# Three staggered streams, per-batch norms and early-divided attention in a four-layer graph network

## The chip, the cores and the metric

The kernel runs on one core of a Trainium2 chip. The metric is device time in microseconds (us) of one execution. Five engines matter below: TensorE (PE; its weight loads are listed apart as PEld), VectorE (DVE), ScalarE (ACT), GpSimd (POOL), and SyncE (SP), which issues the transfers of x and of the result. Each has its own queue of instructions. TensorE has a granted clock, shown as a share of full speed. All timed runs quoted here are in the fast state.

## The reference, cut to what matters

128 batches of 128 nodes with 512 features go through four layers. Each is `x = layernorm(x + layer(x))`, with a shared 128 x 128 matrix `adj`:

```python
# layer 0
y = einsum('nm,bmd->bnd', adj, x);  out = y @ weight + bias
# layer 1: graph attention, one head
h = x @ W
e = leaky_relu((h @ a1)[:, :, None] + (h @ a2)[:, None, :]) * adj
out = elu(softmax(e) @ h + beta * h)
# layer 2: with adj for both weights this reduces to one maximum per row
out = max over m of relu((adj @ x)[o, m] + b[o])
# layer 3: attention with 8 heads of 64, masked where adj == 0
q, k, v = x @ w_qkv
o = softmax(q k^T / 8 + mask) v @ w_proj + b_proj
out = o + (layernorm(o) * gamma + beta3)
```

Everything is fp32. The layer norm is a mean, a variance, and a power of -0.5.

## The kernel before

A group is four batches. `front` takes a group through layers 0 to 2, `back` through layer 3, and the two are stepped in turn, so that two neighbouring groups are in flight. The parts that the argument touches (cuts marked `# ...`):

```python
def interleave(*runs):
    runs = [r for r in runs if r is not None]
    while runs:
        runs = [r for r in runs if next(r, StopIteration) is not StopIteration]

def mean_rstd(st):                      # all four batches of a group at once
    mv = small.tile([P, G, 2], F32, name="mv")
    for b in range(G):
        nc.vector.bn_aggr(mv[:, b, :], st[:, b, :])
    ve = small.tile([P, G], F32, name="ve")
    nc.vector.tensor_scalar(ve, mv[:, :, 1], EPS, None, op0=ALU.add)
    rstd = small.tile([P, G], F32, name="rstd")
    nc.gpsimd.tensor_tensor(rstd, ve, neghalf, op=ALU.pow)
    return mv, rstd

# front, layer 1: scores as 32 products with two columns, mixing after the product
ps = ps_mm.tile([P, G, 2], F32, name="mm")
for b in range(G):
    for k in range(K):
        nc.tensor.matmul(ps[:, b, :], xT[:, k, b * P : (b + 1) * P], wa[:, k, :], ...)
# ... softmax of the four batches' weights e; h = x @ w1; eT = e transposed
for b in range(G):
    p = ps_mm.tile([P, D], F32, name="mm")
    nc.tensor.matmul(p, eT[:, b, :], h[:, b, :], start=True, stop=True)
    # ... elu, residual, stats
mv, rstd = mean_rstd(st)
for b in range(G):
    normalised(xs[:, b, :], xs[:, b, :], mv, rstd, b)

# back, layer 3: one exponential for all heads; the division comes after the values
nc.vector.tensor_tensor(pr, pr, nmx[:, :, None].to_broadcast([P, H, P]), op=ALU.add)
nc.scalar.activation(pr, pr, AF.Exp)
# ... pr transposed to prT
for j in range(2):
    for c in range(K):
        nc.tensor.matmul(pov[:, j, c, :], prT[:, j * K + c, :], ve[:, 2 * c + j, :], ...)
nc.vector.reciprocal(rs, pov[:, :, :, HD : HD + 1])   # sums from a column of ones
nc.vector.tensor_tensor(oa..., pov[:, :, :, :HD], rs..., op=ALU.mult)
transposed(oT, oa, 0)

last = None
for g in range(NG):
    interleave(last, front(xs))
    last = back(g, xs)
```

## Time and profile before

| Before | value |
|---|---|
| time, median of 3 runs | 5197.13 us (5194.22 to 5197.48) |
| span of the profiled run | 5207.6 us |
| TensorE busy / idle | 4181.9 / 1025.7 us |
| TensorE waits that the trace names | 1001 us |
| TensorE time at half clock | 1113 us |
| period of one group | about 161 us |

How to read it: TensorE leads, but it is idle for a fifth of the span, and a fifth of its span runs at half clock. The two go together: after a wait of several microseconds its next products are slow. Time at half clock counts all time at that clock, idle included. The page's lines, the two stretches and the chain are shown in the prediction below. One more place of the timeline matters for later (columns: start, length, engine, line, operation, tile out<-in, shapes, count):

```profile
2727.08 3.63 PE L209 MATMUL mm<-wa,xT 128*128 128x2 f32 x32
...
2731.27 2.08 PE L168 MATMUL mm<-xT,wqkv_sb 128*128 128x512 f32 x2
```

The 32 two-column products follow one another without a gap, yet the two instructions that come soon after take 2.08 us, where two take about 1.0 elsewhere. The clock record has half clock from 2731.2 to 2734.6. TensorE was never idle here; it only had little to multiply. Over all 32 groups the two instructions take 2.07 to 2.08 us in 22 and 1.12 in nine; the first group ran at half clock from before. So the half clock need not be a matter of gaps alone.

### The profile page before, as it was taken

The page shows a single profiled execution, that of the slowest core. Times are in us where ns is not written, and L with a number is a line of the kernel's source. Part 1 is how long each engine was busy: PE and PEld are TensorE (multiplying, and loading weights), DVE is VectorE, ACT ScalarE, POOL GpSimd, SP SyncE. Part 2 cuts the span into 40 slices and gives each one's busy share as a digit, 9 for nine tenths or more (in the row PEclk, how much of TensorE's full clock was granted, in tenths as well). Part 3 has the DMA queues.
Part 4 walks back from the last instruction along what each step waited for, and adds up shares of the span by engine and source line. Part 5 has one row for each costly group of instructions (what it writes and reads, how often), then busy time and mean ns, then how long its engine had stood idle before and what let it go on. Part 6 is the DMA issues. An engine that isn't in the chain of part 4 may idle for free.

```text
span 5207.6 us, 39770 instructions
## 1 busy us (share of the span) xinstructions
PE 4181.9 (80%) x15617; PEld 2305.4 (44%) x15617; DVE 2328.6 (45%) x4243; ACT 942.9 (18%) x1697; POOL 814.7 (16%) x682
## 2 busy tenths in 40 slices
PE   6897777987779877788777887777987779877796
PEld 3454444544444444444444454444544445444443
DVE  3434454434444444544445444454344444444444
ACT  1121111211111111112111121111211111111111
POOL 1111111111110111101111111111111110111101
PEclk8898888988889988899888898888988889988898
DMA  2000000000000000000000000000000000000000
GB/s 85 0 17 17 17 17 9 8 17 17 17 17 1 17 17 17 17 0 17 17 17 17 0 17 17 17 16 8 9 17 17 17 17 1 17 17 17 9 0 17
DMA packets 37242, 77.58 MB, mean 15 GB/s; under 512 B 1472, under 2 KB 1600, under 8 KB 37056
## 3 DMA queue, kind: packets, MB, share of 16 engines
q1 hardware_dynamic: 33936, 67.18, 3.6%
q10 hardware_dynamic: 3120, 7.87, 0.4%
q8 instruction: 124, 2.03, 0.2%
q14 instruction: 62, 0.51, 0.0%
HBM read 41.49 MB, written 33.55 MB: 14 GB/s over the span
## 4 chain that ended last, share of the span: by engine, by line
PE 68%; DVE 18%; POOL 4%; ACT 3%; issue 2%; POOLq 0%; ACTq 0%; DVEq 0%
PE mm L168 52%; DVE st L137 4%; PE tr L161 4%; PE sc L355 3%; PE tr L179 3%; DVE x L387 3%; POOL rstd L146 2%; PE mm L209 2%; PE sc L321 2%; DVE x L150 2%; POOL m L386 2%; DVE oa L362 2%; DVE x L257 1%; ACT oT L162 1%; PE mm L254 1%
## 5 line engine op out<-in xcount | busy, mean ns | idle before, releaser
L168 PE MATMUL mm<-xT,wqkv_sb 128*128 128x512 f32 x2048 | 952.7, 609 | 0.7 <-ACT xT L162 0.7
L161 PE MATMUL tr<-ident,x 128*128 128x128 f32 x1024 | 181.4, 308 | 609.0 <-DVE x L150 609.0
L385 POOL TENSOR_TENSOR x<-x,o 128x512 f32<-128x512 f32 x128 | 162.2, 1267 | 3198.0 <-DVE o L369 3198.0
L168 PE MATMUL mm<-wproj_sb,oT 128*128 128x512 f32 x1024 | 570.4, 708 | 37.5 <-ACT oT L162 37.5
L168 PEld LDWEIGHTS mm<-xT,wqkv_sb 128*128 128x128 f32 x2048 | 385.1, 196 | 410.5 <-issue 406.5
L168 PE MATMUL mm<-w_sb,yT 128*128 128x512 f32 x1024 | 463.7, 596 | 12.7 <-ACT yT L183 12.7
L161 PEld LDWEIGHTS tr<-ident,x 128*128 128x128 f32 x1024 | 146.7, 162 | 734.1 <-issue 733.5
L168 PE MATMUL mm<-w_sb,xT 128*128 128x512 f32 x1024 | 469.2, 601 | 0.0
L168 PE MATMUL mm<-wqkv_sb,xT 128*128 128x512 f32 x1024 | 463.6, 595 | 0.0
L355 PE MATMUL sc<-v_ext,prT 128*128 128x65 f32 x2048 | 283.0, 286 | 156.4 <-DVE prT L348 117.8
L168 PEld LDWEIGHTS mm<-wproj_sb,oT 128*128 128x128 f32 x1024 | 220.3, 226 | 313.6 <-issue 244.0
L192 DVE TENSOR_TENSOR x<-mm,x 128x512 f32<-128x512 f32 x128 | 88.5, 692 | 604.3 <-PE mm L168 363.8
L137 DVE BATCH_NORM_STATS2 st<-x 128x6 f32<-128x512 f32 x512 | 335.5, 680 | 6.3 <-ACT x L281 0.8
L355 PEld LDWEIGHTS sc<-v_ext,prT 128*128 128x128 f32 x2048 | 257.9, 199 | 178.9 <-DVE prT L348 126.6
L306 DVE COPY qkT<-mm 128x512 f32<-128x512 f32 x128 | 88.4, 690 | 527.6 <-PE mm L168 527.6
L150 DVE TENSOR_SCALAR x<-x,mv,rstd 128x512 f32<-128x512 f32 x512 | 248.8, 539 | 144.2 <-POOL rstd L146 144.2
L168 PEld LDWEIGHTS mm<-wqkv_sb,xT 128*128 128x128 f32 x1024 | 191.9, 190 | 253.1 <-issue 229.6
L326 DVE TENSOR_TENSOR pr<-sc,maskb 128x1024 f32<-128x1024 f32 x128 | 156.7, 1224 | 324.4 <-PE sc L321 323.9
L369 DVE TENSOR_TENSOR o<-mm,bproj_sb 128x512 f32<-128x512 f32 x128 | 88.5, 691 | 468.0 <-PE mm L168 463.7
L146 POOL TENSOR_TENSOR rstd<-ve,neghalf 128x4 f32<-128x4 f32 x160 | 162.1, 1013 | 815.8 <-DVE ve L144 815.7
L168 PEld LDWEIGHTS mm<-w_sb,xT 128*128 128x128 f32 x1024 | 190.1, 191 | 222.2 <-issue 214.7
L168 PEld LDWEIGHTS mm<-w_sb,yT 128*128 128x128 f32 x1024 | 190.0, 193 | 213.6 <-issue 200.6
(72 smaller groups left out, 4709.4 us busy)
## 6 DMA issues: line engine op xcount, KB each, us to landing
x<-in_x SPq DMA_DIRECT2D x32, 1024.0 KB, 5.2
out<-x SPq DMA_DIRECT2D x32, 1024.0 KB, 4.3
wqkv_sb<-in_L_gnn_w_qkv ACTq DMA_DIRECT2D x1, 3072.0 KB, 15.2
w_sb<-in_L_gnn_weight ACTq DMA_DIRECT2D x1, 1024.0 KB, 5.7
w_sb<-in_L_gnn_W ACTq DMA_DIRECT2D x1, 1024.0 KB, 12.4
wproj_sb<-in_L_gnn_w_proj ACTq DMA_DIRECT2D x1, 1024.0 KB, 17.5
a_sb<-in_L_gnn_a ACTq DMA_DIRECT2D x1, 512.0 KB, 14.0
bias_sb<-in_L_gnn_bias ACTq DMA_DIRECT2D x1, 256.0 KB, 7.5
```

The costliest lines, as they stand in the source:

```text
L137: nc.vector.bn_stats(st[:, b, :], src)
L146: nc.gpsimd.tensor_tensor(rstd, ve, neghalf, op=ALU.pow)
L150: nc.vector.tensor_scalar(dst, src, mv[:, b, 0:1], rstd[:, b : b + 1], op0=ALU.subtract, op1=ALU.mult)
L161: nc.tensor.transpose(p[:, k, :], src[:, k * P : (k + 1) * P], ident)
L168: nc.tensor.matmul(p, lhs(k), rhs(k), start=(k == 0), stop=(k == K - 1))
L179: nc.tensor.matmul(p[:, k, :], xs[:, b, k * P : (k + 1) * P], adjT, start=True, stop=True)
L209: nc.tensor.matmul(ps[:, b, :], xT[:, k, b * P : (b + 1) * P], wa[:, k, :], start=(k == 0), stop=(k == K - 1),)
L321: nc.tensor.matmul(sc[:, j, c, :], qkT[rws, c, nodes], qkT[rws, K + c, nodes], start=True, stop=True,)
L326: nc.vector.tensor_tensor(pr, sc.rearrange("p j c m -> p (j c) m"), maskb[:, None, :].to_broadcast([P, H, P]), op=ALU.add,)
L355: nc.tensor.matmul(pov[:, j, c, :], prT[:, j * K + c, :], ve[:, 2 * c + j, :], start=True, stop=True,)
L385: nc.gpsimd.tensor_tensor(xs[:, b, :], xs[:, b, :], o[:, b, :], op=ALU.add)
L387: nc.vector.tensor_tensor(xs[:, b, :], xs[:, b, :], ln, op=ALU.add)
```

## The change

Its intent is to keep TensorE fed. (1) `front` ends after layer 1, a new `middle` holds layer 2 and the projections to q, k and v, and three groups are in flight, interleaved by weights. (2) Norms are taken batch by batch. (3) Layer 1's scores become two multiply-and-sum steps on VectorE, and its attention mixes the nodes before the product with w1. (4) Layer 3 divides the attention rows before they are transposed, with the exponential's own sums, and the values become the stationary operand in halves of 64 columns, so that the result comes out already transposed. The diff, cut to its core:

```diff
-def interleave(*runs): ...
+def merge(streams):                       # (generator, total weight)
+    live = [[gen, total, 0.0] for gen, total in streams]
+    while live:
+        s = min(live, key=lambda s: s[2] / s[1])
+        done = next(s[0], None)
+        if done is None:
+            live.remove(s)
+        else:
+            s[2] += done
 # pools: x 3 -> 5 buffers, small 4 -> 6, PSUM tr 2 -> 3, mm 2 -> 3, sc 2 -> 1
+    def mean_rstd(src):                    # one batch
+        nc.vector.bn_stats(st, src)
+        nc.vector.bn_aggr(mv, st)
+        nc.vector.tensor_scalar(ve, mv[:, 1:2], EPS, None, op0=ALU.add)
+        nc.gpsimd.tensor_tensor(rstd, ve, neghalf, op=ALU.pow)      # [P, 1]
 # layer 0, per batch
+            layernorm_act(xs[:, b, :], xs[:, b, :])                 # normalises on ScalarE
+            for i in range(2):
+                nc.vector.scalar_tensor_tensor(
+                    scr, xs[:, b, :], 1.0, wa_rows[:, i, :], op0=ALU.mult, op1=ALU.mult,
+                    accum_out=s[:, b, i : i + 1])
 # layer 1
+        e0 = weights_of(0)                 # two batches
+        yield 0.25
+        e1 = weights_of(1)
+        yield 0.25
+        eTs = [transposed_weights(e0), transposed_weights(e1)]
+        yield 0.5
+        yT = mixed(xs[:, 0, :], eTs[0][:, 0, :])
+        yield 1
+        for b in range(G):
+            nxt = mixed(xs[:, b + 1, :], eTs[(b + 1) // 2][:, (b + 1) % 2, :]) ...
+            p = product(lambda k: yT[:, k, :], lambda k: w1_sb[:, k, :])
+            # ... elu, residual, layernorm_act
 # layer 3
+            for i in range(H):
+                nc.scalar.activation(pr[:, i, :], pr[:, i, :], AF.Exp,
+                    bias=nmx[:, i : i + 1], accum_out=sums[:, i : i + 1])
+            nc.vector.reciprocal(rs, sums)
+            nc.vector.tensor_tensor(pr, pr, rs[:, :, None]..., op=ALU.mult)
 # ... transposes of pr
-                    nc.tensor.matmul(pov[:, j, c, :], prT[:, j * K + c, :], ve[:, 2 * c + j, :], ...)
+                    nc.tensor.matmul(p[j * HD : (j + 1) * HD, c, :],
+                        v[:, b, (2 * c + j) * HD : (2 * c + j + 1) * HD],
+                        prT[:, j * K + c, :], start=True, stop=True)
 # the last loop
+    for i in range(NG + 2):
+        streams: back(i - 2) with 29, middle(i - 1) with 54, front(i) with 41
+        merge(streams)
```

> **What bounds the kernel now.** I read the page's busy shares first, then the clock row, the table of stretches, the waits of TensorE, and last the chain of waits around one group boundary.
>
> ```profile
> span 5207.6 us, 39770 instructions
> PE 4181.9 (80%) x15617; PEld 2305.4 (44%) x15617; DVE 2328.6 (45%) x4243; ACT 942.9 (18%) x1697; POOL 814.7 (16%) x682
> PEclk8898888988889988899888898888988889988898
> ```
>
> No engine is full. TensorE leads at 80%, but its clock averages under 0.9, so even the 80% is inflated by slow matmuls. The kernel is 32 like groups of four batches. Four stretches covering two neighbouring groups show where each loses time (columns: busy of PE, PEld, DVE, ACT, POOL with counts, clock, DMA):
>
> ```profile
> 2520.00:2640.00 120.00, 114.92 (x448) 63.91 (x449) 45.34 (x74) 25.00 (x46) 14.04 (x12) 0.97 0.03 9
> 2640.00:2680.00 40.00, 14.34 (x42) 6.91 (x40) 26.80 (x60) 4.40 (x7) 11.38 (x10) 0.70 0.07 27
> 2680.00:2800.00 120.00, 114.51 (x447) 63.77 (x448) 45.35 (x74) 25.00 (x46) 13.62 (x12) 0.97 0.03 9
> 2800.00:2840.00 40.00, 14.76 (x42) 7.09 (x42) 26.95 (x59) 4.40 (x7) 11.67 (x10) 0.71 0.07 26
> ```
>
> For 120 us TensorE is nearly full at clock 0.97. Then for 40 us it works 14, while VectorE works 27. The waits of TensorE name that hole:
>
> ```profile
> PE tr L161 <- DVE x L150: 609.0, 33, 19.4
> PE sc L355 <- DVE prT L348: 117.8, 62, 3.1
> PE tr L161 <- DVE oa L362: 93.1, 97, 2.8
> PE tr L161 <- DVE mv L142: 47.7, 31, 1.5
> ```
>
> 609 us is one wait of 19.4 us per group: the layer-3 transposes of the new group wait for layer 2's norm, while the old group's last norms, which hold all four batches in lockstep, sit in the same VectorE queue. The chain of waits gives the prices at both clocks (start, length, what):
>
> ```profile
> 2634.92 3.71 PE mm L168 x8
> ...
> 2650.58 6.46 PE mm L168 x8
> ...
> 2678.69 1.02 POOL rstd L146
> ...
> 2688.92 0.89 PE tr L179 x8
> ...
> 2694.58 17.17 PE mm L168 x40
> ...
> 2727.24 3.47 PE mm L209 x32
> ```
>
> An fp32 matmul counts as two instructions here, so a product of four chunks is x8. Dense, it takes 17.17/5 = 3.43 us; after the waits at a group's end the same eight take 6.46. A period is 161 us (the long transpose wait ends at 2680.4 and, fifteen groups on, at 5094.7).
>
> **What the Trainium skill says.** "TensorE: Matmul & The Clock Gate", section "What's actually happening": the array's clock is halved after an idle window of about 3.4 us and released after a busy one. The trace agrees: 3.43 against 6.46 us. "Perfetto Trace Analysis", "Optimization Strategy": where the most contended engine changes over time, interleave those regimes. That is this change; the 40 us stretch is the other regime. "SBUF — State Buffer", "Who interferes with whom": a VectorE instruction with two SBUF inputs contends with a GpSimd one that reads SBUF. The trace agrees: the residual adds at L387, issued beside GpSimd multiplies, have a median of 1.21 us and a minimum of 0.68. "TensorEngine Tiling (Array Packing)", "Key Properties": tiles work independently, but changing the tiling mode drains the array. The row-split scores show the first half (16 in 1.09 us, 68 ns each, where 128 moving columns cost 17.17/160 = 107 ns); no run shows the column form yet.
>
> **The change part by part.** TensorE, per group at full clock, from the chain's rows. Before: 24 products x 3.43 = 82.4; mixing in layer 1 and layer 2, 8 x 0.86 = 6.9; adjacency mixing 4 x 0.89 = 3.6; transposes of x and of the attention output 12 x 0.44 = 5.3; the 2-column score products 3.5; score and weight transposes 1.3; probability transposes 8 x 0.44 = 3.5; layer-3 scores 4 x 1.09 = 4.4; values 4 x 2.01 = 8.0. Sum 119. Busy was 129 of 160 (114.5 + 14.8), so some 10 us is slow clock and 31 us idle.
>
> The change removes the 2-column products (3.5), layer 1's transposes of x (1.8) and of the attention output (1.8), and layer 1's after-mixing (3.4); it adds four mixings of 0.89 (3.6). The values become stationary in 64-column halves with 128 moving columns: between 1.1 us a batch, if halves overlap as the scores do, and 1.7 if not; I take 1.5 against 2.0. Sum 110: minus 9 us a group, all on the path.
>
> VectorE per group, counted in the new order and priced with the old rows: 20 statistics x 0.68, 20 aggregates x 0.16, 20 epsilon adds and 8 small products x 0.17, 8 normalisations x 0.54, 8 score reductions of layer 1 x 0.89 (0.81 plus the accumulator's read), layer-1 weights 5.2, elu and layer-2 max 8.1, small maxima 0.8, copies 5.6, layer-3 softmax 4 x 3.87 = 15.5, add of bias 2.8, gamma and rstd steps 5.4, first add 2.8. Sum 79, against 72 before. So VectorE gains a little work and stays under TensorE.
>
> The norm's power on GpSimd is now per batch: 20 a group instead of 5. Each made VectorE wait 1.1 us before (144.2 + 36.2 us over 160). The new order puts the consumer right behind in about two cases of three: up to 22 us of waits. 79 + 22 = 101 us, below 110 but close, and it lengthens every chain. GpSimd itself: 12 adds x 1.27 + 20 x 1.0 = 35. ScalarE: 32 head-wise exponentials at 0.39 + 0.19 instead of 4 at 1.06 (18.5 against 4.2), 8 normalisations; sum about 49. Neither is a bound.
>
> The wait of 19.4 us should vanish: layer 2's norms now go batch by batch, beside the products of two other groups. But I followed one steady period along the fixed order of each queue, adding those durations, and new waits appear. (a) Layer 1's weights: between the transposes of s and those of e TensorE has just one batch of scores (1.1 us), while VectorE does ten small steps, four exponentials run, and layer 3's mask add and maximum (2 x 1.22) stand in between: about 6.3 us idle, then 1.4 for the copies. (b) Layer 2: max, ScalarE add, statistics, power, normalisation stand behind a whole layer-3 softmax in VectorE's queue; waits of 2.6, 1.1, 1.7 and 2.1 us before transposes, scores, values and projection, about 7.4. (c) 1.5 before the transposes of s. Sum 16.6. About 30 handovers that I did not price: 3 us. After (a), and in the thin 20 us of (b), the clock should fall: 5 us, half of the 10 before.
>
> Period: 110 + 16.6 + 3 + 5 = 134.6; I take 133, since VectorE steps that don't depend on each other start 0.60 apart where I charged 0.68. Staggering costs at the ends: 30 full steps, and four partial ones: front alone about 66 (load included), front and middle 95, middle and back 86, back alone 55. 30 x 133 + 302 = 4292; I put 4270.
>
> **The rivals.** First: TensorE really becomes dense, as the writer intends. For it: three streams always have products ready, and there are three PSUM buffers for two. Against it: the queues are in order, and at (a) the order has no product. It would give 113 x 30 + 280 = 3670 to 3850. Second: VectorE becomes the bound. For it: 101 us with power waits, contention with GpSimd on two-input steps, and the softmax sitting ahead of the norms. Against it: in the stretch after the transposes of s its load is 33 of 50 us by my count. It would make the period some 145, 4650. Third: the column halves drain the array each time they alternate with full products (the order splits them 1 and 7 between products), and cost more than the old form; 1 to 3 us a group, 30 to 100 in all. Fourth: the 19 us wait only moves to another place, the period stays near 155 and the ends add 100: 4950; the batch-wise norms speak against it.
>
> **Range and chances.** The 9 us of removed work are certain, 19 us of wait almost so; what is open is the size of the new waits. A period of 126 gives 4080, one of 140 gives 4500. So 4270, with 4080 to 4480 in eight of ten cases. Faster by over 2%: 0.97; within 2%: 0.02; slower: 0.01.
>
> **What would show it.** Right: TensorE about 85% busy at a clock near 0.94; its longest repeated wait is for layer 1's weight rows (about 6 us, 30 times); no wait over 8 us repeats; VectorE about 60% busy, with some 500 waits for the power near 1 us; values' 16 instructions in 1.1 to 1.7 us; a period of 126 to 140. Wrong: a TensorE wait for layer 2's norm that stays over 5 us, VectorE above 75%, or values' instructions over 2 us a batch. If the period is under 120, my waits (a) and (b) were overcounted.

## The result

| | before | after |
|---|---|---|
| time, median (4 runs each, same rounds) | 5195.68 us | 3976.28 us (3975.49 to 3977.98) |
| ratio after / before (95% interval) | | 0.7653 (0.7642 to 0.7663) |
| TensorE busy / idle | 4181.9 / 1025.7 us | 3709.0 / 265.0 us |
| TensorE waits that the trace names | 1001 us | 250 us |
| TensorE time at half clock | 1113 us | 240 us |
| period of one group | about 161 us | 122.0 us |

A ratio is the mean time of one kernel's fast runs over that of the other's fast runs of the same rounds, so it is not quite the ratio of the medians quoted. The period is the spacing of the transfers of finished groups.

The change is faster by far, and by more than predicted: 3976 us lies below the whole range, 4080 to 4480. The page of the changed kernel:

```profile
span 3974.0 us, 40482 instructions
...
PE 3709.0 (93%) x14345; PEld 1949.2 (49%) x14345; DVE 2382.4 (60%) x5205; ACT 1330.6 (33%) x3777; POOL 925.9 (23%) x1031
...
PEclk9999999999999999999999999999999999999998
```

TensorE is 93% busy instead of 80%, and the clock row that swung between 8 and 9 is level. Two neighbouring periods in the table of stretches (columns as in the prediction):

```profile
2002.00:2124.00 122.00, 115.38 (x448) 60.76 (x448) 74.23 (x163) 41.52 (x118) 28.97 (x33) 0.97 0.05 18
2124.00:2246.00 122.00, 115.83 (x448) 60.94 (x448) 73.82 (x162) 41.52 (x118) 28.55 (x33) 0.97 0.05 17
```

The other regime, 40 us per group with TensorE a third busy, is gone. What is left are 6.4 us of idle TensorE in each 122 (244 less 231.2, halved) and about 2.3 us of slow clock. That last is an estimate: the best kernel below does the same products at clock 1.00 in 113.3 us of busy time, against 115.6 here. The one with a product in the gap does them in 112.0, which would make it 3.6; why these two differ was not traced. The waits of TensorE (total us, times, longest):

```profile
PE tr L238 <- DVE e L230: 133.6, 32, 4.2
PE sc L320 <- DVE qkT L305: 30.8, 32, 1.0
PE tr L287 <- DVE x L164: 16.8, 33, 1.8
```

The wait of 19.4 us per group is gone. Only one of the repeated waits is long: 4.2 us before the transposes of layer 1's weights. TensorE's timeline there:

```profile
2062.74 0.64 PE L208 MATMUL tr<-ident,s 128*128 128x128 f32 x4
2063.30 1.16 PE L320 MATMUL sc<-qkT 64*128 64x128 f32 x16
2068.70 1.39 PE L238 MATMUL tr<-ident,e 128*128 128x128 f32 x4 [4.23 <-DVE e L230]
2069.96 3.78 PE L177 MATMUL tr<-eT,x 128*128 128x128 f32 x16
```

Between the transposes of s and those of e stands nothing but one batch of scores, as the order had shown. After the gap the 16 mixings take 3.58 us from their start to the start of the next row, twice their 1.78 at full clock. VectorE in the same stretch shows what TensorE waits for:

```profile
2063.16 0.76 DVE L212 TENSOR_TENSOR z<-tr,s 128x256 f32<-128x256 f32 x2 [0.16 <-PE tr L208]
...
2065.83 1.21 DVE L325 TENSOR_TENSOR pr<-sc,maskb 128x1024 f32<-128x1024 f32 x1
...
2067.07 1.22 DVE L330 TENSOR_REDUCE nmx<-pr 128x8 f32<-128x1024 f32 x1
2068.21 0.60 DVE L230 SCALAR_TENSOR_TENSOR e<-e,rs,beta_id 128x128 f32<-128x128 f32 x2
```

The eight small steps on e take 2.67 us (2063.16 to 2065.83), two at a time in about 0.67. Then layer 3's mask add and maximum, 1.2 us each, stand in the queue ahead of the last step on e.

Where did the 1234 us between the two spans go? Idle TensorE fell by 761 (62%). Of the fall in busy time, 473 us, I split off the removed work by the count of the prediction: 119 us x 32 groups = 3808 before, 113.3 x 32 = 3626 after, so 182 us (15%); the rest, 291 us (24%), is slow clock that is gone. The last two are estimates, since 119 is a count from single rows and 113.3 is another kernel's busy time.

### The profile page after: what moved, and what is told of

Read it like the earlier page. It is cut to its first block, busy times and chain, and to the rows that moved or that the text cites. A ratio compares the mean times of both kernels' runs of the same rounds, so it can differ in the third digit from the quotient of the medians.

```text
span 3974.0 us, 40482 instructions
## 1 busy us (share of the span) xinstructions
PE 3709.0 (93%) x14345; PEld 1949.2 (49%) x14345; DVE 2382.4 (60%) x5205; ACT 1330.6 (33%) x3777; POOL 925.9 (23%) x1031
## 4 chain that ended last, share of the span: by engine, by line
PE 75%; DVE 15%; POOL 4%; ACT 4%; issue 2%; DMA 1%; ACTq 0%; POOLq 0%; SPq 0%; DVEq 0%
PE mm L170 55%; PE tr L177 7%; PE tr L358 4%; PE mm L275 3%; POOL rstd L153 3%; PE tr L349 2%; DVE st L147 2%; ACT pr L333 2%; DVE x L164 2%; DVE pr L325 2%; DVE nmx L330 2%; PE sc L320 1%; PE tr L238 1%; PE tr L287 1%; DVE pr L339 1%
## 5 line engine op out<-in xcount | busy, mean ns | idle before, releaser
L170 PE MATMUL mm<-w_sb,yT 128*128 128x512 f32 x2048 | 942.3, 598 | 2.1 <-ACT yT L179 2.1
L153 POOL TENSOR_TENSOR rstd<-ve,neghalf 128x1 f32<-128x1 f32 x640 | 417.8, 653 | 2191.2 <-DVE ve L151 1749.5
L170 PEld LDWEIGHTS mm<-w_sb,yT 128*128 128x128 f32 x2048 | 379.7, 195 | 392.3 <-issue 389.9
L160 ACT ACTIVATE x<-x,nmr,rstd 128x512 f32<-128x512 f32 x256 | 208.6, 815 | 920.9 <-DVE nmr L159 920.9
L333 ACT ACTIVATE pr<-pr,nmx 128x128 f32<-128x128 f32 x1024 | 398.9, 393 | 175.2 <-DVE nmx L330 175.2
L191 POOL TENSOR_TENSOR x<-x,bias_sb 128x512 f32<-128x512 f32 x128 | 182.1, 1423 | 182.7 <-PE tr L177 182.6
L358 PEld LDWEIGHTS tr<-prT,v 128*64 128x64 f32 x2048 | 133.2, 137 | 177.8 <-ACT prT L353 87.4
L196 DVE SCALAR_TENSOR_TENSOR scr<-x,wa_rows 128x512 f32<-128x512 f32 x256 | 166.8, 689 | 85.6 <-ACT x L160 85.6
L358 PE MATMUL tr<-prT,v 128*64 128x128 f32 x2048 | 194.7, 283 | 21.3 <-DVE prT L351 12.6
L320 PE MATMUL sc<-qkT 64*128 64x128 f32 x2048 | 182.3, 295 | 34.4 <-DVE qkT L305 30.8
L164 DVE TENSOR_SCALAR x<-x,mv,rstd 128x512 f32<-128x512 f32 x256 | 168.9, 660 | 72.0 <-POOL rstd L153 62.4
```

Source lines behind the costliest of these rows:

```text
L160: nc.scalar.activation(dst, src, AF.Identity, bias=nmr, scale=rstd)
L164: nc.vector.tensor_scalar(dst, src, mv[:, 0:1], rstd, op0=ALU.subtract, op1=ALU.mult)
L170: nc.tensor.matmul(p, lhs(k), rhs(k), start=(k == 0), stop=(k == K - 1))
L191: nc.gpsimd.tensor_tensor(xs[:, b, :], xs[:, b, :], bias0_sb, op=ALU.add)
L196: nc.vector.scalar_tensor_tensor(scr, xs[:, b, :], 1.0, wa_rows[:, i, :], op0=ALU.mult, op1=ALU.mult, accum_out=s[:, b, i : i + 1],)
L320: nc.tensor.matmul(sc[:, j, c, :], qkT[rws, c, nodes], qkT[rws, K + c, nodes], start=True, stop=True,)
```

## The experiments

Two questions were open. First, what made the changed kernel faster than predicted? My theory: the waits were priced from durations that don't hold in the new kernel, the power on GpSimd and the exponentials on ScalarE first. The rival: the durations are right, and three streams hide waits that a walk along the queues doesn't see hidden. Second, which part made the gain? One theory: the third stream, with the rest as decoration. The rival: each part is needed, because each puts back waits of the same kind.

Twelve kernels ran, all correct, all fast. Ratios are to the kernel before in the same rounds, whose median was 5208 to 5212 us on those three chips, so kernels are compared by ratios and not by medians of different chips. "Against changed" is the ratio divided by 0.7653. Waits and half clock are of TensorE, over the whole span; half clock again counts idle time too.

| kernel | median us | ratio | against changed | period us | waits us | half clock us |
|---|---|---|---|---|---|---|
| changed | 3976 | 0.7653 | 1 | 122.0 | 250 | 240 |
| two streams | 4306 | 0.8265 | 1.080 | 130 to 135 | 369 | 500 |
| norms in lockstep | 4320 | 0.8291 | 1.083 | 133 | 504 | 625 |
| mixing after the product | 4053 | 0.7781 | 1.017 | 124.6 | 280 | 292 |
| old attention | 4359 | 0.8366 | 1.093 | 134.2 | 455 | 612 |
| late division alone | 4319 | 0.8288 | 1.083 | 133.1 | 358 | 579 |
| power on four columns | 4118 | 0.7902 | 1.033 | 126.3 | 380 | 309 |
| exponentials spaced out | 4007 | 0.7690 | 1.005 | 122.9 | 284 | 261 |
| both old prices | 4174 | 0.8011 | 1.047 | 126 to 130 | 405 | 368 |
| a product in the gap | 3791 | 0.7277 | 0.951 | 116.0 | 169 | 59 |
| weights early | 3784 | 0.7263 | 0.949 | 116.0 | 123 | 45 |
| weights early, front first | 3885 | 0.7456 | 0.974 | 119.4 | 182 | 164 |
| weights early, middle first | 3827 | 0.7343 | 0.959 | 117.4 | 152 | 46 |

### Undoing one part: two streams

```diff
+    def tail(g):
+        held[g] = []
+        yield from middle(xs[g], held[g])
+        yield from back(g, xs[g], *held[g][0])
-    for i in range(NG + 2):
+    for i in range(NG + 1):
-        # back(i - 2) and middle(i - 1) as streams of their own
+        if i >= 1: streams.append((tail(i - 1), MIDDLE + BACK))
```

> Two streams: the middle and the back of a group run one after the other beside the next group's front, as in the kernel before; batch-wise norms and all else stay. Theory A (it is the batch-wise norms that took the long wait away; a second stream of products is enough to cover them): 3930 to 4030 us. Theory B (the third stream is what covers layer 2 and the softmax): 4200 to 4450 us, with waits of TensorE in layer 2 and in the scores that the three-stream kernel lacks.

It took 4306 us, 8.0% more. The longest wait is now the layer-2 norm, in the waits of TensorE:

```profile
PE tr L287 <- DVE x L164: 102.2, 70, 6.0
```

That wait was 16.8 us in all with three streams. The half clock doubled. The wait at layer 1's weights, on the other hand, is down to 9.8 us in all. The third stream is worth 8%, not the whole gain of 23%: with two streams the kernel still beats the one before by 17%.

### Undoing one part: norms in lockstep

```diff
-            layernorm_act(xs[:, b, :], xs[:, b, :])      # per batch, layers 0 and 1
+            nc.vector.bn_stats(st[:, b, :], xs[:, b, :])
+        norm4_act(xs, st)                                # four batches, one power [P, 4]
# layer 2 likewise with norm4_dve; layer 3 keeps its norms per batch
```

> Three streams kept; the norms of layers 0, 1 and 2 are again taken for four batches together (one power each), those of layer 3 stay batch-wise. Theory A (batch-wise norms took the wait away): 8 to 15 us more a group, 4200 to 4450 us. Theory B (streams alone do it, any norm hides behind two other groups): 3960 to 4040 us.

4320 us, 8.3% more. The waits of TensorE:

```profile
PE tr L329 <- DVE x L184: 143.6, 31, 5.5
PE tr L277 <- DVE e L269: 120.8, 32, 3.8
PE tr L247 <- DVE scr L237: 95.6, 126, 5.6
```

The first and the third are the hole of the kernel before, now small: the transposes of layer 2 wait for the group's norm, and those of s for layer 0's. The middle one, at e, is the changed kernel's own.

### Undoing one part: mixing after the product

```diff
-        eTs = [transposed_weights(e0), transposed_weights(e1)]   # before the products
+        for b in range(G):
+            # transposes of x, product with w1, copy to h
+        eTs = [transposed_weights(e0), transposed_weights(e1)]
+        for b in range(G):
+            nc.tensor.matmul(p, eTs[b // 2][:, b % 2, :], h[:, b, :], start=True, stop=True)
```

For space some work tiles have one buffer here instead of two, and the small pool five instead of six; what that costs was not measured apart.

> Layer 1 again multiplies first and mixes afterwards; the scores still come from VectorE. TensorE has 1.6 us more a group by count (transposes 1.8 and after-mixing 3.4 for 3.6). Theory 1 (the 4.2 us wait is there because mixing ahead leaves no product that does not need the weights): wait and slow clock go, 1.6 - 6.8 = -5 us a group, about 3820 us. Rival (the wait stays, or the added copies and transposes cost more): 4020 to 4080 us.

4053 us, 1.7% more. The wait at e is gone from the list, as a theory of the gap has it: four products now stand between the weights and their transposes. But layer 1's results then come in one burst, four mixings in a row, and the waits move to layer 2:

```profile
PE mm L284 <- ACT x L160: 65.6, 64, 3.8
PE tr L296 <- ACT xT L297: 53.5, 30, 2.2
```

So mixing ahead of the product causes the 4.2 us gap in this interleaving (two streams, and the early weights below, mix ahead too and lose 9.8 and 5.1 us there over the whole run), and is still the better order. The theory was right about the wait and no guide to the sum: it said 3820 us, and the rival's 4020 to 4080 came true.

### Undoing one part: the old attention, and late division alone

```diff
 # old attention
-            # eight exponentials with sums; reciprocal; division of pr
+            nc.vector.tensor_tensor(pr, pr, nmx[:, :, None]..., op=ALU.add)
+            nc.scalar.activation(pr, pr, AF.Exp)
-                    nc.tensor.matmul(p[j * HD : ..., c, :], v[...], prT[...])
+                    nc.tensor.matmul(p[:, c, :], prT[:, j * K + c, :], v[:, b, 2 * c + j, :])
+                nc.vector.reciprocal(rs, p[:, :, HD : HD + 1])
+                nc.vector.tensor_tensor(oav[:, j], p[:, :, :HD], rs..., op=ALU.mult)
+            # four transposes of oa
 # late division alone: the eight exponentials with sums stay; pr is not divided;
 # values, multiplication by rs and four transposes as above
```

In both, the scratch tile of layer 0's scores has one buffer.

> Layer 3's attention as in the kernel before (one exponential over all heads, values moving with a column of ones, rows divided at the end, output transposed), all else as changed. By the change's trace the column halves cost 1.78 us a batch with their alternation, against 2.01, and the four output transposes 1.76 a group go: so 2.7 us more a group, about 4055 us (4030 to 4090). Rival three of the prediction (the column halves drain the array and cost more than the old form): 3976 us or less.

> As changed (exponentials by head with their sums), but the rows are divided after the values' product, which is in the old form (128 stationary columns, 64 moving), and the output is transposed. The full return to the old attention cost 383 us where the count said 80. If the late division is the cause (TensorE, VectorE, TensorE again in the middle of a batch, and a fuller VectorE queue): most of it, 4250 to 4380 us. If the one exponential over all heads with VectorE's subtraction before it was: 3990 to 4100 us.

The old attention took 9.3% more, late division alone 8.3%. So the eight separate exponentials instead of one are worth about 1%, and dividing early with stationary values nearly all of it. My count by work had put the old form only 2.7 us a group higher, some 80 us; it cost 383. The old attention's waits of TensorE:

```profile
PE tr L244 <- DVE e L236: 161.0, 62, 4.1
PE sc L326 <- DVE pr L331: 133.5, 31, 4.6
PE tr L359 <- DVE prT L350: 93.1, 33, 3.4
```

Late division puts a step from TensorE to VectorE and back to TensorE in the middle of each batch. It also puts that step in VectorE's queue, and everything behind it waits longer: the mask add that frees the only score buffer, the copies of the transposed rows, the weights of layer 1. By the list of waits, the order of the queue costs more than the operations; no run tested this by itself, and the split of the 383 us between the two effects was not measured.

### The prices of the prediction put back: power, exponentials, both

```diff
 # power on four columns
-        nc.vector.tensor_scalar(ve, mv[:, 1:2], EPS, None, op0=ALU.add)
+        nc.vector.tensor_scalar(ve, mv[:, 1:2].to_broadcast([P, G]), EPS, None, op0=ALU.add)
-        return mv, rstd
+        return mv, rstd[:, 0:1]          # neghalf, ve and rstd are [P, 4]
 # exponentials spaced out, after each of the eight
+                nc.scalar.copy(sums[:, i : i + 1], sums[:, i : i + 1])
 # both old prices: the two edits together
```

> The changed kernel with the power on four columns (1.0 us in place of 0.55), nothing else. Both prices together cost 198 us. If the norms' chains set the waits, most of that is here: 4080 to 4170 us; if the softmax does, under 4050 us.

> The changed kernel with a one-column copy after each head's exponential (0.48 us apart in place of 0.38), nothing else. If the softmax's chain sets the waits, 4050 to 4130 us; if the norms' chains do, under 4020 us.

> The changed kernel with two of the prices that the prediction used: the power on four columns (1.01 us before, 0.55 as changed) and each head's exponential followed by a one-column copy, so that they start near 0.58 us apart in place of 0.38; no product is added. Theory (the new waits were overcounted because I charged recorded durations and the four-column power, while the work really starts closer together): waits in layer 2 and at layer 1's weights grow, 3 to 8 us a group, 4060 to 4230 us. Rival (these chains are hidden behind the other streams at either price): 4010 us or less.

These experiments compute the same result. The power has the duration that I had charged; the exponentials go only half of the way: with the copies they start 0.48 us apart, where I had charged 0.58 and the changed kernel has 0.38. The records of the power, min/median/max in ns, in the kernel before, in the changed one, and with both old prices:

```profile
L146 POOL TENSOR_TENSOR rstd<-ve,neghalf x160: 1006/1017/1021, 49.7 to 5199.2; 128x4 f32<-128x4 f32 x160
```
```profile
L153 POOL TENSOR_TENSOR rstd<-ve,neghalf x640: 540/550/1004, 33.4 to 3967.6; 128x1 f32<-128x1 f32 x160
```
```profile
L155 POOL TENSOR_TENSOR rstd<-ve,neghalf x640: 1002/1009/1479, 34.7 to 4161.7; 128x4 f32<-128x4 f32 x160
```

By the medians, one column takes 0.55 us and four take 1.01 (one column's mean is 0.65, as some take up to 1.00). I had charged the new one-column power with the old four-column row. And ScalarE's exponentials in the changed kernel (the timeline):

```profile
2005.59 0.40 ACT L333 ACTIVATE pr<-pr,nmx 128x128 f32<-128x128 f32 x1 [0.46 <-DVE nmx L330]
2005.90 0.19 ACT L333 ACTIVATION_READ_ACCUMULATOR pr<-pr,nmx 128x1 f32 x1
2005.99 0.39 ACT L333 ACTIVATE pr<-pr,nmx 128x128 f32<-128x128 f32 x1
```

I had added 0.39 and 0.19 to 0.58; the third row starts 0.40 after the first, and the following ones are 0.38 to 0.39 apart. Records overlap: the next exponential starts before the accumulator read ends.

The power alone costs 3.3%, the spacing alone 0.5%, both together 4.7%: 4174 us, inside the predicted range, though near its lower end. On the changed kernel's chip 4.7% is some 186 us, of the 294 us between my number and the result. The costs don't add up, which is a warning for the four undone parts too. The waits of TensorE with both old prices:

```profile
PE tr L240 <- DVE e L232: 131.6, 33, 4.2
PE sc L322 <- DVE qkT L307: 63.9, 32, 2.1
PE tr L210 <- DVE scr L198: 52.4, 33, 5.4
```

Over 32 groups the third line is 1.6 us before the transposes of s: the prediction's term (c), 1.5, which the changed kernel doesn't have. The wait before the scores doubles to 2.0. So the rival alone falls: had three streams hidden those waits, longer powers would have cost nothing. But the wait at e stays at 4.2, where I had 6.3 and 1.4 for the copies. These prices don't touch it: its eight small steps run 0.33 us apart, where the record of one lasts about 0.42, and layer 1's own four exponentials, which no experiment spaced out, also start 0.39 apart where I had charged 0.58. That is argued from the timeline and was not tested, and so is what is left elsewhere.

### The gap at layer 1's weights: a product in it, and weights early

```diff
 # a product in the gap
         e1 = weights_of(1)
-        yield 0.25
+        yield 4                          # FRONT 41 -> 44.75
 # weights early: the first pair's weights start in layer 0, the second's in layer 1
+            if b == 2:                   # loop of layer 0
+                e0 = weights_of(0)
+        eT = transposed_weights(e0)
+            if b == 0:                   # loop of layer 1
+                e1 = weights_of(1)
+            elif b == 1:
+                eT = transposed_weights(e1)
+                nxt = mixed(xs[:, 2, :], eT[:, 0, :])
```

> The changed kernel, with products of the other two streams put between layer 1's score transposes and its weight transposes. Theory 1 (the 4.2 us wait of each group is only a missing piece of TensorE work at that place, and the slow clock after it is its consequence): the wait goes, and with it some 2.6 us of halved clock, 6.5 us a group, so about 3780 us. Rival (VectorE is behind at this place, and the wait turns up before the next consumer): 3930 to 3980 us.

> The changed kernel, with layer 1's weights of the first two batches made while layer 0 of the last batch still runs, and those of the other two while the first two are multiplied. If the wait at the weights is a matter of order alone, it goes without the softmax standing before it: 3740 to 3790 us. If VectorE's queue is what ends it, no better than the filled version, 3790 to 3850 us.

One number in the weights of the interleaving lets another stream run a product where TensorE was idle. TensorE's timeline of the kernel with a product in the gap:

```profile
2079.98 3.60 PE L170 MATMUL mm<-xT,wqkv_sb 128*128 128x512 f32 x8
2083.51 1.16 PE L320 MATMUL sc<-qkT 64*128 64x128 f32 x16
2086.74 0.50 PE L238 MATMUL tr<-ident,e 128*128 128x128 f32 x2 [2.07 <-DVE e L230]
```

And VectorE's:

```profile
2084.01 0.55 DVE L164 TENSOR_SCALAR x<-x,mv,rstd 128x512 f32<-128x512 f32 x1 [0.44 <-POOL rstd L153]
2086.24 0.61 DVE L230 SCALAR_TENSOR_TENSOR e<-e,rs,beta_id 128x128 f32<-128x128 f32 x2
2087.82 1.22 DVE L325 TENSOR_TENSOR pr<-sc,maskb 128x1024 f32<-128x1024 f32 x1
```

The product covers 3.5 us, but the wait falls only from 4.2 to 2.1. Layer 3's softmax is no longer what stands ahead of e: its mask add comes at 2087.82, after the last step on e (2087.29). In its place layer 2's norm (from its statistics at 2081.77 to L164 at 2084.01) now stands among the small steps. But the period falls by 6.0 us, more than the wait: the shorter gap no longer slows the clock, and half clock falls from 240 us to 59. Taking the weights early removes the wait altogether (5 us over the whole run, in two places) and makes the fastest kernel of the study, 3784 us, 27% under the one before and 5% under the changed one. A stretch of one of its periods:

```profile
1884.00:2000.00 116.00, 113.34 (x450) 58.72 (x449) 74.14 (x162) 41.20 (x119) 28.95 (x32) 1.00 0.05 19
```

TensorE works 113.3 of 116.0 us at full clock. From here only less work on TensorE can give much more: with no idle time at all a group would still take 112 to 113.

### The order of the streams: front first, middle first

```diff
-        merge(streams)                   # weights early, front first
+        merge(streams[::-1])
 # weights early, middle first: middle is appended ahead of back
```

> As the early version, and each step starts with the front's stream in place of the back's, so that the first scores of a group don't follow directly on the last copy of q and k (1.0 us of TensorE wait a group as changed): 30 us less than the early version, 3710 to 3760 us. Rival: the wait is only moved, same as the early version.

> The early version, with each step starting with the middle's stream, so that a layer-2 product stands between the last copy of q and k and the first scores. If the 1.0 us wait of each group is only that gap: 3750 to 3765 us. Rival (the order decided by the start shifts other waits in, as in the version that starts with the front): 3785 us or more.

The aim was the wait of 1.0 us before the scores, which wait for the last copy of qkT. It goes in both, and both are slower, by 101 and 43 us. With front first the waits of TensorE are led by

```profile
PE tr L289 <- DVE mv L149: 65.4, 31, 2.7
PE sc L322 <- DVE pr L327: 41.2, 34, 3.0
```

These two make 107 us, in exchange for the one of 31; since some other waits shrank, all waits together rose from 123 to 182, and the half clock from 45 to 164. With middle first the new ones are smaller (oT 32.8, prT 27.9, pr 25.6 us). This theory missed: the order of ties had been worth more than the wait that I could name.

### What the four undone parts say together

The parts cost 329, 344, 77 and 383 us, together 1133, near the whole gain of 1219 us. That sum is no proof of independence, as the powers and the exponentials show, and the medians are from different chips, some 0.3% apart. It does say that no single part made the gain. Two of the four leave TensorE's products as they are, so what they add is waiting and slow clock alone: two streams 119 us more wait and 204 us more busy time (3913 against 3709), norms in lockstep 254 and 86. The part that is undone differs, the currency is the same, and the third stream by itself does not decide it.

## Why the prediction was right or wrong

**Direction and mechanism: right.** It gave 0.97 to faster by over 2%, and the ratio is 0.765. The 19.4 us wait vanished, as it said. The longest repeated wait is where it said, at layer 1's weights, about 30 times (32), with no wait over 8 us repeating. VectorE is 60% busy as predicted, and the ends of the pipeline cost 3974 - 30 x 122.0 = 314 us, where it had 302.

**The failed step: the sum of the new waits.** The mechanism was right and the size was not. Its terms, in us per group:

| term of the prediction | predicted | measured |
|---|---|---|
| TensorE work at full clock | 110 | 113.3 (112.0 in one kernel) |
| (a) layer 1's weights, with the copies after | 6.3 + 1.4 | 4.2, copies near 0 |
| (b) layer 2 behind layer 3's softmax | 7.4 | about 2.2 |
| (c) before the transposes of s | 1.5 | near 0 |
| handovers not priced | 3 | in the above |
| slow clock | 5 | 2.3 |
| period | 134.6, taken as 133 | 122.0 |

The waits measured are 6.4 in all, against 16.6 + 3. The 30 steady periods times 11.0 us account for 330 us; the ends take back 12. That is 318 us from the sum of the working, 4292; the number on record was set 22 us lower, at 4270, without a reason given, so its error is 294.

The reason that the runs showed: prices taken from rows of another shape or read as if they didn't overlap. "Each made VectorE wait 1.1 us before" was true of a power on four columns. With one column VectorE waited for it 456 times (225 + 104 + 127 in the three consumers), 275 us in all, 0.6 each; the number of waits, some 500, was right and the "near 1 us" was not. "0.39 + 0.19" was right as two records and wrong as a spacing. Putting the power back in full and the spacing by half returned the time to the predicted range. By time that is 186 of 294 us, and the power alone some 130 of them. Of the rest, term (a) holds 3.5 us a group by the table, which the old prices leave as it was. The waits before layer 2's transposes were 0.5 us where I had 2.6, and the old prices bring back only 0.8 of the difference (to 1.3). Why those two came out short was read from the timeline, not shown by a run.

**Slow clock: right in place, half in size.** The products just after (a) account for it: the 16 mixings lost 1.8 us, the four transposes before them some 0.8 (1.26 from start to start, against 0.44). The thin 20 us of (b), where I had let the clock fall as well, were not thin enough: the clock record has one stretch of half clock in each steady period, 3.4 or 6.8 us long, and it is the one at (a).

**Work: 2 to 3.3 us too low.** The removed work is some 6 to 7 us, not 9. The values took 1.78 us a batch with the alternation to full products and back, where I took 1.5. In one batch the 16 values and the 8 product instructions among them cover 2078.03 to 2083.24, 5.21 us; the product alone takes 3.43. That is 1.1 us of four batches; the rest was not traced.

**Rival 1, a dense TensorE (3670 to 3850): nearer than my own number.** The changed kernel lies between the two. Its objection, that at (a) the order has no product, held. Giving it one reached 3791 us, and moving the weights 3784, both in that range.

**Rival 2, VectorE as the bound: wrong** as a throughput bound, at 60%. As the place that the waits come from it is in nearly every line shown. **Rival 3, the drain: true but small**, inside the 1.78 us. **Rival 4, the wait only moves: wrong** for the change; it came true in miniature in three of the experiments (mixing after the product and the two orders).

**The shape of the page** was predicted as 85% busy at clock 0.94; it is 93% at 0.97. The sign that it set for its own failure, "under 120, my waits (a) and (b) were overcounted", was put at too low a period: they were overcounted at 122.

## What to carry to other kernels

Price a moved operation from a row with its own shape, and a run of instructions by the distance between starts, not by the sum of the records: here the two, tested together, made more than half of the error, most of it by the shape of the power. When TensorE leads and is not full, look for the place where its queue has no product between a step and the step's consumer, and put a product of another stream there; one number in the weights of the interleaving gave 4.9%, nearly all of the 5.1% that the best order reached. A wait of TensorE that is long enough to halve the clock costs more than itself: shortening one from 4.2 us to 2.1 was worth 6.

## What the Trainium skill lacked or had wrong

- "GPSIMD Engine Reference" gives no duration for a small power. Here 128 x 1 takes 0.55 us and 128 x 4 takes 1.01 (medians), so for the reciprocal root of a norm the number of columns counts even at this size.
- "TensorE: Matmul & The Clock Gate", section "What's actually happening", names an idle window as what halves the clock. In the kernel before, 32 two-column products without a gap (3.63 us) were followed by two instructions that took 2.08 us instead of about 1.0; so a window full of instructions with little array work can have the same effect. Of the 32 groups, 22 showed it; in five of these the products themselves already ran slow at their end (4.8 us), and in nine groups the two took 1.12. The page has something like it for transposes only, in another section: they do not count as busy in the same way.
- "TensorEngine Tiling (Array Packing)", section "Key Properties", says that a change of tiling mode drains the array, with no number. Here a batch of column-half values that alternates with full products takes 1.78 us, less than the 2.0 of the form without the halves; by an estimate from the same rows (16 at the 72 ns of the 14 that run together make 1.15, and there are four changes of mode) a change costs about 0.15 us.
- "Perfetto Trace Analysis", section "DVE / Act Engine Instruction", says that the recorded end is the acknowledgement of the write. The same page says further on that this part overlaps with the next instruction, and the runs agree. What no page gives is the figure for an exponential with an accumulator read: records of 0.39 and 0.19 us, but 0.38 from start to start.
